# Transposed columns of the first image's lower half moved from the first stage into layer 0, and a step order of four for two images

## The chip, the cores and the metric

The kernel runs on one core of one Trainium2 chip. The metric is the device time of one execution in microseconds. Times "before" are of three runs; the profile is one more execution, taken by the hardware profiler.

## The reference, cut to what matters

The input x is 4 images of 16 channels, 256 x 256. Two layers, each a residual around a normalisation and a convolution:

```python
x = x + _L0_conv_ref(_gn(x), conv_w, conv_b)
x = x + _L1_conv_ref(_gn(x), base_w, spline_w, spline_scaler, bias)

def _L0_conv_ref(x, conv_w, conv_b):          # x is already normalised
    out = conv3x3(x, conv_w) + conv_b         # 16*25 output channels
    weights = softmax(out.reshape(N, C, 25, H, W), axis=2)
    return einsum('ncuij,ncuij->ncij', unfold5x5(x), weights)

def _gn(v, G=8, eps=1e-5):                    # over pairs of channels of an image
    g = v.reshape(B, G, C // G, H, W)
    return ((g - mean(g)) / sqrt(var(g) + eps)).reshape(v.shape)
```

Layer 1 is a 3 x 3 convolution of spline features and of silu of the normalised x. The change doesn't touch it.

## The kernel before, in words

**First stage (L404 to L589).** All 8 half images (4 images, 128 rows each) are loaded (`load_x`, L415; the two halves of image 0 stay in `held`, the others share three buffers). For each half DVE takes the statistics (L534, L536), ACT the squares (L543), PE sums them (L546), DVE takes the maximum (L549). After each image `group_stats` gives mean and deviation (with one power on POOL, L154). After the last image a flag is made (L580 to L589) which bounds the logits; every engine branches on it, and one of two equal arms runs (L1116).

Beside this the first image is normalised by the generator `normalize` (L264), two or three steps of which are taken after each piece of the statistics (L540, L541, L550). The order of instructions on each engine in this stage is chosen by a scheduler from what the program issues; it is not the order of the source.

**What `normalize` makes.** It works through four groups of four channels (q). `rows(q)` (L317) makes, for each half h, two forms of the normalised x on ACT: `hsp`, strips with a border of two columns (L327), stored in `hs` by `put_rows`, and `ht`, the same values reordered for the transposes (L340). `columns(q, n, h)` (L349) makes one tile of the transposed image: four PE transposes to PSUM (`tp`, L362), a copy `tt` (by DVE in the first stage, by ACT otherwise, L355), a copy `hi` rounded to float32r (ACT, L355), and the difference `lo` = `tp` - `hi` (DVE, L370). Each tile has 130 rows: a half with one row of the other half as border, for which 128x4 copies are made (L357, L359, and `border`, L311, for `lo`). There are 4 x 2 x 2 tiles for an image. `put_columns` (L294) stores `tt`, `hi`, `lo` of both halves in `hst` and `hsl`, six stores of 260 KB for each (q, n). Stores and loads are put in a list `moves` with the number of steps by which they are late. In this kernel a tile takes six steps: transposes, copies, difference, three empty ones.

Images 1, 2 and 3 are normalised in the same way during the layer 0 of the image ahead of them; there x comes into two tiles `xp` (`load`, L278), one for each half.

**Layer 0 (L620 to L883).** 64 strips (4 images, 2 halves, 8 strips of 32 columns), 8 steps of four columns each. In a step PE makes the logits (L833 from `am`, which is read from `hst`; L837 from `an`, which is read from `hsl`), ACT the exponentials `e` (L856), POOL the products with the neighbourhood `u`, read from `hs` (L861), DVE the sums of numerators and denominators (`nd`, L700), one step later. `e` has four buffers, `lg` three, `am`/`an` three; an `am` block serves two steps and is loaded two blocks ahead (L819). Once a strip DVE divides (L720 to L722), POOL subtracts (L728). After that comes one step of `normalize` (L870). Within layer 0 each engine's instructions run in the order of the source (`in_order`, L591). All these loads and stores are issued by SP on one queue.

**Layer 1 (L886 to L1110)** follows on all engines.

Of the kernel before, what the change touches and what calls it, by code (L numbers as in the profile page):

```python
# [3 lines left out]

# [7 lines left out]
F32 = mybir.dt.float32  # L12
F32R = mybir.dt.float32r
AF = mybir.ActivationFunctionType
# [20 lines left out]
def conv_preact_kernel(  # L35
# [12 lines left out]
    nc = tc.nc  # L48
    B, C, H, W = x.shape
    G = 8  # L50
    GC = C // G
    P = 128
    NH = H // P
# [3 lines left out]
    PAD = K // 2  # L57
# [3 lines left out]
    SW = 32  # L61
    NST = W // SW
    SP = SW + 2 * PAD
# [4 lines left out]
    RP = P + 2  # L68
    CT = (W + 2) * RP
    QC = 4  # L70
    QW = W // (P // QC)
    QG = 4
# [8 lines left out]
    const = ctx.enter_context(tc.tile_pool(name="const", bufs=1))  # L81
# [42 lines left out]
    for r in range(RT):  # L124
        p = P // 2 + SROWS.index(r + 1) * C
# [118 lines left out]
    zpad = const.tile([P, QC, PAD], F32, name="zpad")  # L244
    nc.vector.memset(zpad, 0.0)

    def zeros(b, queue):

        for e in (0, HP - PAD):
            for r in range(PAD):  # L250
                yield partial(
                    queue.dma_start,
                    hs[b][:, e + r].rearrange("s c w -> c s w"),
                    zero[0:C, 0 : NST * SP].rearrange("c (s w) -> c s w", s=NST),
                )
        for h in range(NH):
            for w in (0, (W + 1) * RP):
                yield partial(queue.dma_start, hst[b][h][:, w : w + RP], zero[0:C, 0:RP])
                yield partial(
                    queue.dma_start,  # L260
                    hsl[b][h][:, :, w : w + RP].rearrange("c t r -> (c t) r"), zero[:, 0:RP],
                )

    def normalize(b, ptr, tiles, held=None, copier=None):  # L264

        prep, xps, tts, his, los = tiles
        copier = copier or nc.scalar.copy

        moves = [(20 + 4 * i, f) for i, f in enumerate(zeros(b, nc.sync))] if held is None else []

        def move():
            for f in [f for i, f in moves if i <= 0]:
                f()
            moves[:] = [(i - 1, f) for i, f in moves if i > 0]

        def load(q, h):  # L278
            if held is None and q < C // QC:
                nc.sync.dma_start(  # L280
                    xps[h][:, :, PAD : PAD + W],
                    x[b, q * QC : (q + 1) * QC, h * P : (h + 1) * P, :].rearrange(
                        "c p w -> p c w"),
                )

        def put_rows(q, h, hsp):
            r0 = PAD + h * P
            nc.sync.dma_start(
                hs[b][:, r0 : r0 + P, q * QC : (q + 1) * QC, :].rearrange(
                    "s r c w -> r s (c w)"),  # L290
                hsp.rearrange("p s c w -> p s (c w)"),
            )

        def put_columns(q, n):  # L294
            g0 = n * QG
            for h in range(NH):
# [13 lines left out]

        def border(t):  # L311
            nc.scalar.copy(t[:, 1, :, 0:1], t[:, 0, :, P : P + 1])
            nc.scalar.copy(t[:, 0, :, RP - 1 :], t[:, 1, :, 1:2])

        hts = {}

        def rows(q):  # L317
            for h in range(NH):
                xp = xps[h] if held is None else held[h][:, q * QC : (q + 1) * QC]
                hsp = prep.tile([P, NST, QC, SP], F32, name=f"hsp{b}_{q}_{h}", tag="hsp")  # L320
                ht = prep.tile([P, QW, W // QW, QC], F32, name=f"ht{b}_{q}_{h}", tag=f"ht{h}")
                hts[q, h] = ht
                for k in range(QC // GC):
                    g = q * (QC // GC) + k
                    kc = slice(k * GC, (k + 1) * GC)
                    how = dict(scale=nrm[b][:, 0, g : g + 1], bias=nrm[b][:, 1, g : g + 1])
                    nc.scalar.activation(  # L327
                        hsp[:, :, kc, :].rearrange("p s c w -> p c s w"),
                        bass.AP(
                            tensor=xp.tensor, offset=xp.offset + k * GC * (W + 2 * PAD),  # L330
                            ap=[xp.ap[0], [W + 2 * PAD, GC], [SW, NST], [1, SP]],
                        ),
                        AF.Identity, **how,
                    )
                    if k == QC // GC - 1:
                        nc.scalar.copy(hsp[:, 0, :, 0:PAD], zpad)
                        nc.scalar.copy(hsp[:, NST - 1, :, PAD + SW :], zpad)
                        moves.append((4, partial(put_rows, q, h, hsp)))
                    yield
                    nc.scalar.activation(  # L340
                        ht[:, :, :, kc].rearrange("p g w c -> p c w g"),
                        xp[:, kc, PAD : PAD + W].rearrange("p c (w g) -> p c w g", g=QW),
                        AF.Identity, **how,
                    )
                    if k == QC // GC - 1:
                        moves.append((4, partial(load, q + 1, h)))
                    yield

        def columns(q, n, h):  # L349

            tp = ptr.tile([P, QG, P], F32, name=f"tp{b}_{q}_{n}_{h}", tag="tp")

            def copy(t, to):

                to(t[:, h, :, 1 : 1 + P], tp)  # L355
                if h == 0:
                    to(t[:, 1, :, 0:1], tp[:, :, P - 1 :])  # L357
                else:
                    to(t[:, 0, :, RP - 1 :], tp[:, :, 0:1])  # L359

            for k in range(QG):
                nc.tensor.transpose(  # L362
                    tp[:, k, :], hts[q, h][:, n * QG + k].rearrange("p w c -> p (w c)"), ident
                )
            yield
            copy(tts[n], copier)
            copy(his[n], nc.scalar.copy)
            yield

            nc.vector.tensor_sub(  # L370
                los[n][:, h, :, 1 : 1 + P], tp, his[n][:, h, :, 1 : 1 + P].bitcast(F32)
            )
            if h == NH - 1:
                moves.append((5, partial(border, los[n])))
                moves.append((9, partial(put_columns, q, n)))
            yield
            yield
            yield
            yield

        for h in range(NH):
            load(0, h)
        yield
        for _ in rows(0):
            move()
            yield
        for q in range(C // QC):
            ahead = rows(q + 1) if q + 1 < C // QC else iter(())
            for n in range(QW // QG):
                for h in range(NH):  # L390
                    for k, _ in enumerate(columns(q, n, h)):
                        if k % 3 == 2:
                            next(ahead, None)
                        move()
                        yield
            for _ in ahead:
                move()
                yield
        while moves:
            move()  # L400
            yield


    with tc.tile_pool(name="prep0", bufs=2) as prep, tc.tile_pool(  # L404
# [121 lines left out]
        for b in range(B):  # L526
# [44 lines left out]
            if b == 1:  # L571
                prepare1()
            if b == 0:
                ahead = normalize(0, ptr0, tiles, held, nc.vector.tensor_copy)
                next(ahead)
        for _ in ahead:
            pass
# [42 lines left out]
    def layer0(shift):  # L620
# [4 lines left out]
        with tc.tile_pool(name=f"prep{arm}", bufs=2) as prep, tc.tile_pool(  # L625
# [172 lines left out]
            for n, (b, hf, s) in enumerate(strips):  # L798
                if (hf, s) == (0, 0):
                    for _ in ahead:  # L800
                        pass
                    ahead = normalize(b + 1, ptr, tiles) if b + 1 < B else iter(())
                    if b == B - 1:
                        bank = ptr.tile([P, QG, P], F32, name=f"ps{arm}", tag="tp")
                        first_scales = [scales(k, partial(lambda k: bank[:, k], k)) for k in range(2)]
                last = (hf, s) == (NH - 1, NST - 1)
                if last:
                    for _ in ahead:
                        pass
                u = us.pop(0)  # L810
                if s * SW % CX == 0:
# [350 lines left out]
```

## Time and profile before

| | |
|---|---|
| median of three runs | 3069.55 us |
| lowest, highest | 3064.12, 3075.65 us |
| the profiled execution, own time | 3061.86 us |
| its span, first to last instruction | 3059.8 us |
| DVE busy in the span | 2959.0 us (97%) |
| PE busy in the span | 2802.6 us (92%) |
| ACT, POOL busy | 2236.6 us (73%), 1947.6 us (64%) |
| moved by DMA | 626.29 MB |

Times in the trace count from the span's start. A group of instructions is shown as line, engine, operation, output and inputs by the program's names, shapes and count, then the busy time in us and the mean of one in ns, then the idle time of the engine just before them and what ended it. `PEld` is PE's loading of weights. In a list of waits, the columns are who waited for whom, the sum in us, how often, and the longest. The share of DMA is the mean busy share of the core's 16 DMA engines, which can be a little over 1 by the packets' own records.

### The profile page before, as it was taken

The page shows a single profiled execution, that of the slowest core. Times are in us where ns is not written, and L with a number is a line of the kernel's source. Part 1 is how long each engine was busy: PE and PEld are TensorE (multiplying, and loading weights), DVE is VectorE, ACT ScalarE, POOL GpSimd, SP SyncE. Part 2 cuts the span into 40 slices and gives each one's busy share as a digit, 9 for nine tenths or more (in the row PEclk, how much of TensorE's full clock was granted, in tenths as well). Part 3 has the DMA queues.
Part 4 walks back from the last instruction along what each step waited for, and adds up shares of the span by engine and source line. Part 5 has one row for each costly group of instructions (what it writes and reads, how often), then busy time and mean ns, then how long its engine had stood idle before and what let it go on. Part 6 is the DMA issues. An engine that isn't in the chain of part 4 may idle for free.

```text
span 3059.8 us, 39743 instructions
## 1 busy us (share of the span) xinstructions
PE 2802.6 (92%) x14248; PEld 1448.2 (47%) x14248; DVE 2959.0 (97%) x1587; ACT 2236.6 (73%) x2587; POOL 1947.6 (64%) x744
## 2 busy tenths in 40 slices
PE   4499999999999999999999999958999999999998
PEld 3366656656656666666666566632222222222222
DVE  7599999999999999999999999998999999999997
ACT  6466765676766566766646546559999999999996
POOL 4199999999999999999999999980100100000000
PEclk7699999999999999999999999978999999999999
DMA  8988977879878778978767667659999999999994
GB/s 273 290 223 221 258 205 209 222 189 257 234 209 240 196 202 225 248 216 220 212 174 200 164 173 194 161 131 198 201 192 195 198 194 189 198 194 202 190 197 91
DMA packets 350929, 626.29 MB, mean 205 GB/s; under 512 B 41330, under 2 KB 216676, under 8 KB 334852
## 3 DMA queue, kind: packets, MB, share of 16 engines
q1 hardware_dynamic: 318020, 605.29, 81.0%
q10 hardware_dynamic: 30960, 15.73, 1.8%
q0 software_dynamic: 1744, 2.64, 0.3%
q8 instruction: 117, 1.92, 0.3%
q14 instruction: 88, 0.72, 0.1%
HBM read 513.95 MB, written 104.24 MB: 202 GB/s over the span
## 4 chain that ended last, share of the span: by engine, by line
DVE 69%; issue 11%; PE 8%; DMA 3%; ACT 3%; POOL 2%; SPq 1%; DVEq 0%; ACTq 0%; POOLq 0%
DVE nd L700 44%; PE lg L833 6%; DVE ta L168 4%; DVE ta L167 4%; DVE tb L168 4%; DVE tb L167 4%; DVE tb L158 2%; PE lg L837 1%; DVE yo L1020 1%; POOL e L861 1%; DVE r L721 1%; DVE nd L720 1%; DVE lo L370 1%; DMA am<-hst 1%; DVE nd L722 1%
## 5 line engine op out<-in xcount | busy, mean ns | idle before, releaser
L861 POOL TENSOR_TENSOR e<-e,u 128x1600 f32<-128x1600 f32 x512 | 1788.4, 3539 | 49.0 <-ACT e L856 30.9
L833 PE MATMUL lg<-wm,am 128*128 128x400 f32 x4096 | 1734.8, 505 | 83.8 <-ACT e L856 53.0
L700 DVE TENSOR_REDUCE nd<-e 128x128 f32<-128x3200 f32 x512 | 1748.0, 3478 | 29.0 <-POOL e L861 28.9
L837 PE MATMUL lg<-wn,an 97*128 97x400 f32 x2048 | 1344.9, 657 | 17.3 <-DMA an<-hsl 17.3
L856 ACT ACTIVATE e<-lg 128x800 f32<-128x800 f32 x1024 | 818.2, 837 | 708.9 <-DVE nd L700 460.5
L833 PEld LDWEIGHTS lg<-wm,am 128*128 128x128 f32 x4096 | 760.9, 192 | 403.3 <-ACT e L856 98.2
L1037 PE MATMUL yp<-ring,wt 128*32 128x512 f32 x6144 | 745.9, 598 | 87.6 <-DVE ring L169 63.7
L837 PEld LDWEIGHTS lg<-wn,an 97*128 97x128 f32 x2048 | 388.3, 190 | 334.5 <-issue 23.6
L1037 PEld LDWEIGHTS yp<-ring,wt 128*32 128x32 f32 x6144 | 203.7, 109 | 621.7 <-issue 427.7
L954 POOL MEMSET sl<- 16x256 f32 x6 | 1.8, 306 | 402.7 <-ACT ta L163 299.8
L169 DVE SCALAR_TENSOR_TENSOR ring<-ta,ta 128x2048 f32<-128x2048 f32 (+1 forms) x64 | 147.9, 2310 | 2.5
L168 DVE TENSOR_TENSOR ta<-ta,ta 128x2048 f32<-128x2048 f32 (+1 forms) x64 | 147.5, 2305 | 2.8 <-ACT ta L166 2.8
L169 DVE SCALAR_TENSOR_TENSOR ring<-tb,tb 128x2048 f32<-128x2048 f32 x64 | 145.6, 2275 | 2.5
L748 ACT ACTIVATE z<-xc,nrm 128x256 f32<-128x256 f32 x240 | 144.2, 601 | 5.3 <-POOL xc L728 1.2
L168 DVE TENSOR_TENSOR tb<-tb,tb 128x2048 f32<-128x2048 f32 x64 | 145.4, 2271 | 0.0
L1047 PE MATMUL yp<-sl,ws 64*32 64x512 f32 (+1 forms) x1032 | 131.3, 602 | 0.0
L954 POOL MEMSET slc<- 16x256 f32 x2 | 0.6, 307 | 203.1 <-ACT ta L163 203.0
L166 ACT ACTIVATE ta<-ta 128x2048 f32<-128x2048 f32 (+1 forms) x64 | 123.4, 1928 | 2.0
L193 POOL TENSOR_TENSOR d<-d,nrz 128x8 f32<-128x8 f32 x4 | 2.7, 669 | 191.8 <-DVE d L191 191.8
L166 ACT ACTIVATE tb<-tb 128x2048 f32<-128x2048 f32 x64 | 120.6, 1884 | 0.0
L973 ACT ACTIVATE sl<-sl,q 64x2048 f32<-64x2048 f32 x43 | 90.0, 2094 | 1.1
L728 POOL TENSOR_TENSOR xc<-xc,nd 128x512 f32<-128x512 f32 x64 | 82.5, 1289 | 8.2 <-DVE nd L722 8.2
(195 smaller groups left out, 2089.3 us busy)
## 6 DMA issues: line engine op xcount, KB each, us to landing
am<-hst SPq DMA_DIRECT2D x512, 194.6 KB
u<-hs SPq DMA_DIRECT2D x320, 288.0 KB
an<-hsl SPq DMA_DIRECT2D x512, 129.8 KB
xta<-x1s SPq DMA_DIRECT2D x40, 1024.0 KB
xtb<-x1s SPq DMA_DIRECT2D x40, 1024.0 KB
xtc<-x1s SPq DMA_DIRECT2D x40, 1024.0 KB
am<-hst SPq DMA_DIRECT2D x256, 129.8 KB
sl<-x1s SPq DMA_DIRECT2D x166, 128.0 KB
```

The lines of the kernel that those rows point to most:

```text
L166: nc.scalar.activation(s1, r1, AF.Square, scale=2.0)
L167: nc.vector.scalar_tensor_tensor(s2, t, 2.0, s2, ALU.subtract, ALU.mult)
L168: nc.vector.tensor_mul(s1, s1, r1)
L169: nc.vector.scalar_tensor_tensor(f, s2, 0.0, s1, ALU.min, ALU.subtract if given else ALU.add)
L700: nc.vector.tensor_reduce(nd[:, :, :, j : j + JG].rearrange("p t c j -> p t j c"), e.rearrange("p t j m c d -> p t j c m d"), AX.XY, ALU.add,)
L748: nc.scalar.activation(z, v, f, scale=nrm[b][:, 0, g : g + 1], bias=nrm[b][:, 1, g : g + 1], accum_out=st1[b][:, t, g, columns_of(n) : col ...
L833: nc.tensor.matmul(lg[:, i, :NL], lhsT=am[:, o : o + P], rhs=wm.rearrange("p m c d -> p (m c d)"), start=True, stop=False,)
L837: nc.tensor.matmul(lg[:, i, :NL], lhsT=an[:, o : o + P], rhs=wn.rearrange("p m c d -> p (m c d)"), start=False, stop=True,)
L856: nc.scalar.activation(ev, lg[:, :, :NL], AF.Exp)
L861: nc.gpsimd.tensor_tensor(e[:, 1].rearrange("p j m c d -> p j (m c) d"), e[:, 0].rearrange("p j m c d -> p j (m c) d"), uv, ALU.mult,)
L1037: nc.tensor.matmul(yp[t * M : (t + 1) * M], lhsT=wt[:, d, e].rearrange("p r o -> p (r o)"), rhs=ring[:, r0 + t * RT + d : r0 + t * RT + d ...
L1047: nc.tensor.matmul(yp[t * M : (t + 1) * M], lhsT=ws[v, e].rearrange("p r o -> p (r o)"), rhs=sl[n % 3][v, t : t + NT + 1 : NT, e : e + W], ...
```

## The change

`normalize` gets a `part`: None is the whole image, 0 and 1 are the two halves of image 0. In the first stage only part 0 runs: it makes rows and `ht` of both halves and transposes both, but of the lower half's tiles it takes only the border row; the upper half's border row, which the lower half will need, is kept in three small tiles (`kept`, for `tt`, `hi`, `lo`). Part 1 runs in layer 0 of image 0, ahead of image 1's normalisation: it loads the lower half of image 0 again, four channels at a time into the two `xp` tiles in turn and two groups ahead, makes `ht`, transposes, copies, takes the difference and stores three pieces for a tile. With `dense` (part 1, and image 1) transposes, copies and difference of a tile are issued in one step, followed by three empty ones, and a step of `rows` comes in every second step. Images 2 and 3 keep six steps. Stores of part 1 are issued four steps after the difference, not nine.

```diff
+    NQ = QW // QG
+    kept = [
+        const.tile([P, C // QC * NQ, QG, 1], d, name=f"kept{i}") for i, d in enumerate((F32, F32R, F32R))
+    ]
-    def normalize(b, ptr, tiles, held=None, copier=None):
+    def normalize(b, ptr, tiles, held=None, copier=None, part=None, dense=False):
-        moves = [(20 + 4 * i, f) for i, f in enumerate(zeros(b, nc.sync))] if held is None else []
+        moves = [(20 + 4 * i, f) for i, f in enumerate(zeros(b, nc.sync))]
+        moves = moves if held is None and part is None else []
+        parts = range(NH) if part is None else (part,)
+        read = range(NH) if part != 1 else (1,)
+        def place(q, h):
+            return xps[h if part is None else q % 2]
...
-                    xps[h][:, :, PAD : PAD + W],
+                    place(q, h)[:, :, PAD : PAD + W],
...
         def put_columns(q, n):
-            for h in range(NH):
+            for h in parts:
...
         def rows(q):
-            for h in range(NH):
-                xp = xps[h] if held is None else held[h][:, q * QC : (q + 1) * QC]
+            for h in read:
+                xp = place(q, h) if held is None else held[h][:, q * QC : (q + 1) * QC]
...
+                    if part != 1:
                         (hsp as before, with its yield)
...
-                        moves.append((4, partial(load, q + 1, h)))
+                        moves.append((4, partial(load, q + (1 if part is None else 2), h)))
...
-            def copy(t, to):
-                to(t[:, h, :, 1 : 1 + P], tp)
-                if h == 0:
-                    to(t[:, 1, :, 0:1], tp[:, :, P - 1 :])
+            def copy(t, to, keep):
+                if h in parts:
+                    to(t[:, h, :, 1 : 1 + P], tp)
+                if part == 1:
+                    to(t[:, 1, :, 0:1], keep[:, q * NQ + n])
+                elif h == 1:
+                    to(t[:, 0, :, RP - 1 :], tp[:, :, 0:1])
                 else:
-                    to(t[:, 0, :, RP - 1 :], tp[:, :, 0:1])
+                    to(t[:, 1, :, 0:1] if part is None else keep[:, q * NQ + n], tp[:, :, P - 1 :])
...
-            yield
-            copy(tts[n], copier)
-            copy(his[n], nc.scalar.copy)
-            yield
+            if not dense:
+                yield
+            copy(tts[n], copier, kept[0])
+            copy(his[n], nc.scalar.copy, kept[1])
+            if not dense:
+                yield
+            v = slice(1, 1 + P) if h in parts else slice(RP - 1, RP)
+            to = h if h in parts else 0
             nc.vector.tensor_sub(
-                los[n][:, h, :, 1 : 1 + P], tp, his[n][:, h, :, 1 : 1 + P].bitcast(F32)
+                los[n][:, to, :, v], tp[:, :, 0 : v.stop - v.start],
+                his[n][:, to, :, v].bitcast(F32),
             )
+            if part == 0 and h == 0:
+                moves.append((1, partial(
+                    nc.scalar.copy, kept[2][:, q * NQ + n], los[n][:, 0, :, P : P + 1]
+                )))
+            if part == 1:
+                nc.scalar.copy(los[n][:, 1, :, 0:1], kept[2][:, q * NQ + n])
             if h == NH - 1:
-                moves.append((5, partial(border, los[n])))
-                moves.append((9, partial(put_columns, q, n)))
+                if part is None:
+                    moves.append((5, partial(border, los[n])))
+                moves.append((9 if part is None else 4, partial(put_columns, q, n)))
...
-        for h in range(NH):
+        for h in read:
             load(0, h)
+            if part == 1:
+                load(1, h)
         yield
+        if part == 1:
+            yield
...
-                        if k % 3 == 2:
+                        if k in ((1, 3) if dense else (2, 5)):
                             next(ahead, None)
...
-                ahead = normalize(0, ptr0, tiles, held, nc.vector.tensor_copy)
+                ahead = normalize(0, ptr0, tiles, held, nc.vector.tensor_copy, 0)
...
-                    ahead = normalize(b + 1, ptr, tiles) if b + 1 < B else iter(())
+                    ahead = normalize(b + 1, ptr, tiles, dense=b == 0) if b + 1 < B else iter(())
+                    if b == 0:
+                        late = normalize(0, ptr, tiles, part=1, dense=True)
+                        ahead = chain(late, ahead)
...
+                if n == NST - 2:
+                    for _ in late:
+                        pass
```

Lines are those of the kernel before; in the changed kernel the same code stands up to 45 lines later.

More of the change, by code (lines that the diff above doesn't have):

```diff
@@ L2 @@
 from functools import partial
+from itertools import chain
 from itertools import chain
@@ L317, in rows @@
         def rows(q):
-            for h in range(NH):
-                xp = xps[h] if held is None else held[h][:, q * QC : (q + 1) * QC]
-                hsp = prep.tile([P, NST, QC, SP], F32, name=f"hsp{b}_{q}_{h}", tag="hsp")
+            for h in read:
+                xp = place(q, h) if held is None else held[h][:, q * QC : (q + 1) * QC]
+                if part != 1:
+                    hsp = prep.tile([P, NST, QC, SP], F32, name=f"hsp{b}_{q}_{h}", tag="hsp")
                 ht = prep.tile([P, QW, W // QW, QC], F32, name=f"ht{b}_{q}_{h}", tag=f"ht{h}")
@@ L326, in rows @@
                     how = dict(scale=nrm[b][:, 0, g : g + 1], bias=nrm[b][:, 1, g : g + 1])
[L327 to L338, printed above, removed]
-                    yield
+                    if part != 1:
+                        nc.scalar.activation(
+                            hsp[:, :, kc, :].rearrange("p s c w -> p c s w"),
+                            bass.AP(
+                                tensor=xp.tensor, offset=xp.offset + k * GC * (W + 2 * PAD),
+                                ap=[xp.ap[0], [W + 2 * PAD, GC], [SW, NST], [1, SP]],
+                            ),
+                            AF.Identity, **how,
+                        )
+                        if k == QC // GC - 1:
+                            nc.scalar.copy(hsp[:, 0, :, 0:PAD], zpad)
+                            nc.scalar.copy(hsp[:, NST - 1, :, PAD + SW :], zpad)
+                            moves.append((4, partial(put_rows, q, h, hsp)))
+                        yield
                     nc.scalar.activation(
@@ L364, in columns @@
                 )
-            yield
-            copy(tts[n], copier)
-            copy(his[n], nc.scalar.copy)
-            yield
+            if not dense:
[6 more added lines that the diff above has]
+            to = h if h in parts else 0
             nc.vector.tensor_sub(
-                los[n][:, h, :, 1 : 1 + P], tp, his[n][:, h, :, 1 : 1 + P].bitcast(F32)
-            )
+                los[n][:, to, :, v], tp[:, :, 0 : v.stop - v.start],
+                his[n][:, to, :, v].bitcast(F32),
+            )
+            if part == 0 and h == 0:
[4 more added lines that the diff above has]
+                nc.scalar.copy(los[n][:, 1, :, 0:1], kept[2][:, q * NQ + n])
             if h == NH - 1:
-                moves.append((5, partial(border, los[n])))
-                moves.append((9, partial(put_columns, q, n)))
+                if part is None:
+                    moves.append((5, partial(border, los[n])))
+                moves.append((9 if part is None else 4, partial(put_columns, q, n)))
             yield
@@ L379, in columns @@
             yield
-        for h in range(NH):
+        for h in read:
             load(0, h)
+            if part == 1:
+                load(1, h)
         yield
+        if part == 1:
+            yield
         for _ in rows(0):
@@ L389, in normalize @@
             for n in range(QW // QG):
-                for h in range(NH):
+                for h in read:
                     for k, _ in enumerate(columns(q, n, h)):
-                        if k % 3 == 2:
+                        if k in ((1, 3) if dense else (2, 5)):
                             next(ahead, None)
```

## The prediction

> **What bounds the kernel now.** I read the page's slices first, then the same by stretches of 50 us (columns: stretch, then busy us and count of PE, PEld, DVE, ACT, POOL, then granted clock, DMA share, GB/s).
>
> ```profile
> DMA  8988977879878778978767667659999999999994
> ```
> ```profile
> 50.00:100.00 50.00, 27.16 (x115) 22.57 (x115) 38.19 (x111) 43.79 (x63) 3.71 (x4) 0.60 0.90 293
> 100.00:150.00 50.00, 21.70 (x77) 14.15 (x76) 21.60 (x54) 13.32 (x30) 9.87 (x21) 0.67 1.02 284
> 200.00:250.00 50.00, 50.00 (x182) 33.11 (x181) 49.93 (x20) 33.83 (x54) 50.00 (x16) 1.00 0.91 245
> 1650.00:1700.00 50.00, 47.50 (x166) 30.55 (x165) 49.86 (x22) 23.83 (x34) 50.00 (x16) 1.00 0.64 160
> ```
> To 150 us (statistics and the first image's normalisation) the 16 DMA engines are full and no engine is; from 160 to 2040 us (layer 0) DVE has no gap, with POOL and PE close behind. The groups of DVE in one image's layer 0 (165 to 640 us) and all waits of layer 0 say the same: DVE never waits, and what others wait for is mostly DVE.
>
> ```profile
> L700 DVE TENSOR_REDUCE nd<-e 128x128 f32<-128x3200 f32 x128 | 437.2, 3478 | 0.1
> L370 DVE TENSOR_TENSOR lo<-tp,hi 128x512 fp32r<-128x512 f32 x16 | 10.9, 681 | 0.0
> ```
> ```profile
> ACT e L856 <- DVE nd L700: 460.5, 298, 4.5
> ...
> PE lg L833 <- DMA am<-hst: 14.3, 7, 5.2
> ```
> Then the timeline between the stages, by engine (start, length, what, idle before and its releaser).
>
> ```profile
> 120.44 1.87 SPq L648 DMA_DIRECT2D am<-hst  x3
> ...
> 129.75 5.59 SPq L648 DMA_DIRECT2D am<-hst  x1
> ```
> ```profile
> 135.04 0.84 ACT L856 ACTIVATE e<-lg 128x800 f32<-128x800 f32 x1 [0.87 <-PE lg L837]
> 147.17 0.87 ACT L327 ACTIVATE hsp<-xp,nrm 128x576 f32<-128x576 f32 x1 [11.30 <-DMA am<-hst]
> ```
> ```profile
> 136.91 6.97 DVE L700 TENSOR_REDUCE nd<-e 128x128 f32<-128x3200 f32 x2 [16.95 <-POOL e L861]
> 153.11 3.49 DVE L700 TENSOR_REDUCE nd<-e 128x128 f32<-128x3200 f32 x1 [9.23 <-POOL e L861]
> 157.03 3.49 DVE L700 TENSOR_REDUCE nd<-e 128x128 f32<-128x3200 f32 x1 [0.43 <-POOL e L861]
> 161.04 13.96 DVE L700 TENSOR_REDUCE nd<-e 128x128 f32<-128x3200 f32 x4 [0.53 <-POOL e L861]
> ```
> Layer 0's loads begin at 120.44. ACT stands 11.3 us after two steps of exponentials: its next instruction reads the x tiles of image 1 (named am in the wait, but the instruction reads xp), whose loads are behind 3 of am/an, one of u and 1 MB of xc. DVE runs without a break from 161.04 only.
>
> **What the Trainium skill says.** "Perfetto Trace Analysis", section Optimization Strategy: where the most contended engine changes over time, interleaving the regimes may help. The trace agrees on the regimes (DMA 1.02 before 150 us, DVE 49.9 of 50 after), not yet on the gain. The same page, Optimizing Scalar/DVE Operations: the profiled latency holds a half that overlaps the next instruction; here a difference shows 0.68 us, but the next starts 0.60 us after it (below), so I charge 0.60. "DMA: Bandwidth & Descriptors", Issuing engines are not separate DMA queues: all transfers share 16 engines and interleave, so moved stores meet the am loads; the loads already wait for PE or each other, and PE waits 14.3 us for am in 1,880.
>
> **The change, part by part.**
>
> *Taken from the first stage.* For the lower half's 8 tiles: 8 DVE copies and 8 differences, 8 ACT roundings, and 24 stores of 260 KB. The 32 transposes stay there, for the border column (128x4 copies of 0.06 us start to start). DVE: 8 x (0.60 + 0.60) = 9.6 us; ACT: 8 x 0.50 = 4.0 us; stores: 6.4 MB, at the 337 GB/s of 60 to 120 us, 19 us. No one of these is the gain: none is alone on the path. I follow the chain instead, with durations of before and the built order of the changed kernel:
> - SP stood from 45.4 to 59.2 for hsp with stores queued behind it; now the first group of stores is ahead of it. The load of the seventh x half goes out at about 61.5 instead of 64.9 and has fewer stores before it: landed at 72 instead of 75.9.
> - The last x half had 12 stores between it and that load; now 3, so it goes out at about 74 instead of 84.7 and lands at 84 instead of 95.
> - Arrival then no longer decides; ACT's row does: squares of the sixth, seventh and eighth half (3.5 us each) with 1.2 us `ht`, 0.8 us `hsp` and 0.5 us roundings end at about 75, 84 and 91 (before 79.6, 87.2, 99.1).
> - PE's sums of squares at half clock with two transposes between (5.4 us before), held about 3 us by differences that free PSUM: maximum at about 99.6 (before 102.9). From there to the flag 10.5 us in before, less a copy, a difference and a wait for a rounding, 2.8: 107.3 (before 113.4).
> - After the flag came one more tile and 6 stores, to 119.0; now the last stores are out before the flag. First load of layer 0 at about 108 instead of 120.4: 12.5 us. Bounds: 6 (the flag's gain alone) and 17 (stores' DMA time nearly in full).
>
> *The start of layer 0.* Loads keep their order, and image 0's lower x takes the place of image 1's. But in ACT's row no `hsp` comes, and the first `ht` stands after six exponentials, not two, and needs one x tile, not both. The tile lands 23.4 us after the first load (26.7 before, less 2.4 for the second and 0.9 of old stores). `ht` 1.1, two exponentials 1.6, POOL 3.5, the fourth sum 3.5: the fifth sum starts 33.7 us after the first load; before, 161.04 - 120.44 = 40.6. Gain 6.9 us; bounds 2 and 9.
>
> *Added in image 0's layer 0.* 8 differences on DVE, which has no gap: 8 x 0.60 = 4.8 us, all on the path. Copies and roundings go to ACT (8 x 1.3 us, and `ht` 8 x 1.1: 19 us in image 0, where ACT is busy 34 of 50 and otherwise waits for DVE). PE: 32 transposes, 8 x 0.44 = 3.5 us, under its 2 to 4 idle us in 50. SP: 24 stores and 4 loads of 512 KB, 28 x 0.6 = 17 us of issue, under its 548 us of waiting for PE's release of am. If these covers were gone they would cost up to 19, 3.5 and 17 us.
> DMA: 8.5 MB, 25 us at the same rate. Without normalisation the share in layer 0 is about 0.69 (four stretches from 1650: 0.60 to 0.74), in image 0 about 0.85; the difference over an image is some 67 us. Image 1's normalisation now fills about 80 steps of 3.75 us, not 105: 67/300 = 0.22 more, so 0.91. The windows show up to 1.0 without a gap on DVE: cost 0, bounds 0 and 8.
>
> *One step of four.* No instruction more for image 1. New waits: ACT's copies wait for transposes of the same step, DVE's difference for ACT's rounding of the same step. Behind the difference on DVE stands the next sum. The timeline has the distance (the same tile from the transposes to the difference):
>
> ```profile
> 301.42 0.60 PE L362 MATMUL tp<-ident,ht 128*128 128x128 f32 x4
> ...
> 309.28 0.59 ACT L355 CAST hi<-tp 128x512 fp32r<-128x512 f32 x1
> ...
> 321.43 0.68 DVE L370 TENSOR_TENSOR lo<-tp,hi 128x512 fp32r<-128x512 f32 x1
> 322.03 10.26 DVE L700 TENSOR_REDUCE nd<-e 128x128 f32<-128x3200 f32 x3
> ```
> The rounding is done 11.6 us ahead of the difference. One step (3.65) earlier for ACT, two for DVE leave 8 us: cost 0. Transposes reuse PSUM four steps after the difference, as now. On SP the lower half's stores come 4 steps after their difference; next am loads stand behind them, due two blocks (14.6 us) later: cost 0, bounds 0 and 4.
>
> **Sum.** -12.5 - 6.9 + 4.8 = -14.6 us. The profiled execution (span 3059.8, own time 3061.86) becomes 3047.3; the median of the runs, 3069.55, lies 7.7 above it, and becomes 3055. Own range -24 to -4: 3045 to 3065.
>
> **The rivals.** *The first stage doesn't end earlier:* x loads and statistics set it, stores were a shadow. For: SP's stalls are partly ACT's; against: full DMA and the tail after the flag. Only the start's 6.9 remains, less 4.8: 3067. *Crowded DMA:* at 0.91 the am loads come late in bursts; if a tenth of the 67 + 25 us shows on PE and gets through, 9, with the 8 of the bounds above: about -14.6 + 15, 3070. *Same-step waits (slower):* if ACT's lead is below zero at the differences, each of 24 tiles stops DVE for transposes 0.6, copies 1.2 and part of an exponential 0.7: 24 x 2.5 = 60 us, 3115. It decides only once 8 us of lead are lost, for example behind a late store that still reads `hi`.
>
> **How the numbers follow.** Forecast 0.76, no earlier end 0.08, crowded DMA 0.08, same-step waits 0.08. 0.5% is 15.3 us, about what a measurement of this kernel can tell from no change. The forecast's centre is 0.7 us inside that, and what I left at zero lies rather on the gain's side (am and u also land earlier without old stores ahead of them), so a little over half of its 0.76 goes beyond: faster 0.42. The rest, 0.34, and the next two cases, 0.16, make within 0.50; slower 0.08. Range: 3044 to 3070, the last case left out.
>
> **What would show it.** Right: the first am load near 108 us, ACT's first `ht` after six exponentials, DVE gapless from about 142, the same spacing to 2040, an am wait no larger. Wrong: a difference that waits for ACT, PE waiting for am above 15 us, a first load after 115.

## The result, and the profile after

| | before | changed | ratio, 95% interval |
|---|---|---|---|
| median of the runs, us | 3066.84 (3061.70 to 3075.65, 4 runs) | 3047.90 (3045.66 to 3052.85, 4 runs) | 0.9945 [0.9923, 0.9967] |
| the profiled execution: own time / span, us | 3061.86 / 3059.8 | 3052.85 / 3050.8 | one execution each: -9.0 |

The kernel is faster by 19 us in these runs, and by 9 us in the two profiled executions. That is one finding, not two: in these runs the executions of before lie up to 14 us apart, those of the changed kernel 7 us. So the changed kernel was run twice more without an edit, on two different chips, each time beside the kernel before:

| | changed | before | ratio, 95% interval |
|---|---|---|---|
| first repeat | 3049.14 (6 runs) | 3062.06 (43 runs) | 0.9953 [0.9937, 0.9968] |
| second repeat | 3051.24 (12 runs) | 3061.45 (49 runs) | 0.9972 [0.9960, 0.9985] |

The gain is 10 to 19 us by chip (13 and 10 in the repeats), 0.3 to 0.55%. The forecast was 14.6.

Now the views that answer to those of before. First the page's slices (busy share of the DMA engines in 40 slices) and two stretches (stretch, busy us and count of PE, PEld, DVE, ACT, POOL, granted clock, DMA share, GB/s), changed kernel:

```profile
DMA  8988988878978778878857667659999999999993
```
```profile
100.00:150.00 50.00, 33.19 (x100) 20.18 (x100) 25.47 (x40) 18.33 (x27) 23.69 (x25) 0.80 0.88 230
200.00:250.00 50.00, 50.00 (x185) 33.17 (x183) 49.86 (x23) 30.39 (x50) 50.00 (x16) 1.00 0.88 253
```

The regimes are what they were: DVE fills layer 0 (49.9 of 50). What differs is the stretch from 100 to 150 us, in which PE works 33.2 us instead of 21.7 and POOL 23.7 instead of 9.9: layer 0 begins earlier in it. Then SP's queue, ACT and DVE between the stages, changed kernel (start, length, what, idle before and its releaser):

```profile
108.56 1.88 SPq L686 DMA_DIRECT2D am<-hst  x3
...
117.71 0.41 SPq L716 DMA_DIRECT2D xc<-in_x_dram  x1
119.11 5.78 SPq L686 DMA_DIRECT2D am<-hst  x3
```
```profile
134.99 1.27 ACT L359 ACTIVATE ht<-xp,nrm 128x512 f32<-128x512 f32 x1 [6.36 <-DMA am<-hst]
```
```profile
107.31 0.14 DVE L627 CAST flag<-bd 1x1 int32<-1x1 f32 x1
...
124.16 6.97 DVE L738 TENSOR_REDUCE nd<-e 128x128 f32<-128x3200 f32 x2 [12.44 <-POOL e L906]
132.27 3.49 DVE L738 TENSOR_REDUCE nd<-e 128x128 f32<-128x3200 f32 x1 [1.14 <-POOL e L906]
141.27 3.49 DVE L738 TENSOR_REDUCE nd<-e 128x128 f32<-128x3200 f32 x1 [5.51 <-POOL e L906]
144.68 0.68 DVE L396 TENSOR_TENSOR lo<-tp,hi 128x512 fp32r<-128x512 f32 x1
145.28 3.48 DVE L738 TENSOR_REDUCE nd<-e 128x128 f32<-128x3200 f32 x1
149.86 10.48 DVE L738 TENSOR_REDUCE nd<-e 128x128 f32<-128x3200 f32 x3 [1.11 <-POOL e L906]
```

The first load of layer 0 goes out at 108.56 instead of 120.44. ACT's first `ht` stands after six exponentials, as built, and still waits 6.4 us for its x (the wait is named `am`, but the instruction reads `xp`; 11.3 before). DVE's longest break after its first sums is 5.5 us, ahead of the fourth sum; before it was 9.2, ahead of the third. The fifth sum starts at 145.28 instead of 161.04. Last the groups of DVE in image 0 (150 to 625 us) and the waits of all of layer 0 (total us, times, longest), changed kernel:

```profile
L738 DVE TENSOR_REDUCE nd<-e 128x128 f32<-128x3200 f32 x127 | 434.8, 3478 | 2.5 <-POOL e L906 2.5
L396 DVE TENSOR_TENSOR lo<-tp,hi 128x512 fp32r<-128x512 f32 x23 | 15.7, 681 | 0.0
```
```profile
ACT e L901 <- DVE nd L738: 440.7, 290, 4.5
...
PE lg L878 <- DMA am<-hst: 16.0, 8, 5.0
...
ACT hsp L346 <- DMA xp<-in_x_dram: 9.5, 3, 4.2
...
DVE nd L738 <- POOL e L906: 5.2, 6, 1.2
```

The differences have become 23 in this window (the 24th is the one at 144.68), with no idle time ahead of any: none waits for ACT. A line that before did not have is `hsp` waiting for `xp`: where image 1's normalisation begins in the middle of image 0, ACT stands for x.

**Where the time came from.** Shifts of three executions of the changed kernel against the profiled one of before, in us, taken from the starts on SP and DVE:

| | first load | fifth sum | image 1's first sum | last sum of layer 0 | end |
|---|---|---|---|---|---|
| changed | -11.9 | -15.8 | -9.1 | -8.0 | -9.1 |
| first repeat | -12.1 | -17.9 | -13.1 | -13.8 | -15.6 |
| second repeat | -12.5 | -20.4 | -12.5 | -10.8 | -11.0 |
| denser steps alone (an experiment below) | -1.1 | -4.3 | -4.6 | -4.5 | -4.0 |

Against this one execution, all three win 12 us in the first stage and 4 to 8 more by the fifth sum, and give 5 to 8 back in image 0. After image 0 they move by 2.4 us at most.

The last row shows how far one execution of before can be trusted as the zero. Up to the fifth sum the rows of all engines in that kernel's trace are those of before, instruction by instruction, and yet:

```profile
119.35 1.87 SPq L686 DMA_DIRECT2D am<-hst  x3
```
```profile
149.36 3.49 DVE L738 TENSOR_REDUCE nd<-e 128x128 f32<-128x3200 f32 x1 [7.29 <-POOL e L905]
153.28 20.91 DVE L738 TENSOR_REDUCE nd<-e 128x128 f32<-128x3200 f32 x6 [0.43 <-POOL e L905]
```

Its fifth sum (the second of the last row; it starts at 156.76) is 4.3 us earlier than in before, with nothing done for it. Counted from this execution the changed kernel wins 10.8 to 11.4 us in the first stage, but only 0.7 to 4.8 more by the fifth sum. The first stage stands firm: in four executions with the old first stage (two of them from the experiments on the kernel before) the first load goes out at 119.0 to 120.4, in eight with the new one, experiments included, at 108.0 to 109.4, which is 11.1 us apart on average.

### The profile page after: what moved, and what is told of

Read it like the earlier page. It is cut to its first block, busy times and chain, and to the rows that moved or that the text cites. A ratio compares the mean times of both kernels' runs of the same rounds, so it can differ in the third digit from the quotient of the medians.

```text
span 3050.8 us, 39867 instructions
## 1 busy us (share of the span) xinstructions
PE 2804.2 (92%) x14280; PEld 1447.6 (47%) x14280; DVE 2954.8 (97%) x1587; ACT 2252.1 (74%) x2619; POOL 1948.5 (64%) x744
## 4 chain that ended last, share of the span: by engine, by line
DVE 68%; issue 12%; PE 9%; DMA 5%; ACT 3%; POOL 2%; SPq 1%; DVEq 0%; POOLq 0%; ACTq 0%
DVE nd L738 43%; PE lg L878 6%; DVE ta L169 4%; DVE ta L168 4%; DVE tb L169 4%; DVE tb L168 4%; DVE tb L159 2%; PE lg L882 2%; DVE yo L1065 1%; POOL e L906 1%; DVE r L759 1%; DMA an<-hsl 1%; DVE nd L758 1%; DVE nd L760 1%; DVE lo L396 1%
## 5 line engine op out<-in xcount | busy, mean ns | idle before, releaser
L882 PE MATMUL lg<-wn,an 97*128 97x400 f32 x2048 | 1344.3, 656 | 12.8 <-DMA an<-hsl 12.7
L882 PEld LDWEIGHTS lg<-wn,an 97*128 97x128 f32 x2048 | 388.1, 190 | 330.7 <-issue 21.7
```

The costliest lines, as they stand in the source:

```text
L882: nc.tensor.matmul(lg[:, i, :NL], lhsT=an[:, o : o + P], rhs=wn.rearrange("p m c d -> p (m c d)"), start=False, stop=True,)
```

## The experiments

Theory: three terms, as predicted: an earlier end of the first stage, an earlier unbroken row on DVE because ACT asks later for x, less eight differences on DVE. Rivals: the whole gain is the place of ACT's wait, and the first stage a side matter; the denser steps cost or win something by themselves; the stores alone, or the engines' work alone, set the end of the first stage. Each kernel was run in five rounds beside the kernel before.

**The changed kernel again** (first repeat, in the tables above).

> The changed kernel once more, against the kernel before in five rounds, since two profiled executions gave -9 us and the medians of four runs -19. Sum of the forecast's terms as measured in the first trace (first load of layer 0 11.9 us earlier, start of layer 0 2.8 better, 8 differences 4.8, gaps of DVE 1.4): ratio 0.997. If the medians are right: 0.994.

Measured 0.9953 [0.9937, 0.9968]. What follows: differences of a few us between the times of single executions mean nothing. The readings below are mostly of starts on SP and DVE early in the trace, and even these carry the spread shown above.

**Denser steps for image 1 alone**, first stage and image 0 as before:

```diff
-                ahead = normalize(0, ptr0, tiles, held, nc.vector.tensor_copy, 0)
+                ahead = normalize(0, ptr0, tiles, held, nc.vector.tensor_copy)
...
-                        late = normalize(0, ptr, tiles, part=1, dense=True)
-                        ahead = chain(late, ahead)
+                        late = iter(())
```

> Only the step order of four for image 1, nothing moved out of the first stage. If a same-step wait cost 2.5 us a tile, 16 tiles make +40 us (ratio 1.013). My theory: no difference on DVE waits for ACT, ratio 1.000 within 0.002, and the sums of image 0 keep the spacing of the kernel before to within 1 us.

Measured 0.9992 [0.9981, 1.0002] (3059.75 against 3062.06). From the sixth sum to image 1's first, image 0 takes 457.9 us, before 458.2. One step of four by itself costs nothing that these runs can tell, and no difference waits for ACT.

**The lower half's work back in the first stage, without its stores** (eight DVE copies, eight roundings, eight differences, made and not used):

```diff
-                if h in parts:
+                if h in parts or part == 0:
                     to(t[:, h, :, 1 : 1 + P], tp)
...
+            if part == 0 and h == 1:
+                nc.vector.tensor_sub(
+                    los[n][:, 1, :, 1 : 1 + P], tp, his[n][:, 1, :, 1 : 1 + P].bitcast(F32),
+                )
```

> The changed kernel, with the lower half's 8 copies, 8 roundings and 8 differences made in the first stage as well (their result is not used), but not its 24 stores. If the engines' work set the end of the first stage, the first load of layer 0 goes back from 108.6 us to about 116 to 120. If the stores did, it stays within 2 us of 108.6. I expect something between, nearer to the work: 114, 5 us above the changed kernel.

Measured 0.9972 [0.9962, 0.9982], 3053.56, 4.4 above the changed kernel on the same chip (the two intervals overlap a little). The flag and the first load, this kernel:

```profile
112.23 0.14 DVE L631 CAST flag<-bd 1x1 int32<-1x1 f32 x1
```
```profile
113.49 1.87 SPq L690 DMA_DIRECT2D am<-hst  x3
```

The first load is 4.9 to 5.5 us later than in the three executions of the change alone, and so is the flag: it comes 4.9 us later than in the first of them.

**The stores back, without the work** (24 stores of the upper tiles a second time, into spare memory):

```diff
+    spare = dram.tile([C, CT], F32, name="spare"), dram.tile([C, 2, CT], F32, name="sparel")
...
-            for h in parts:
+            for h in range(NH) if part == 0 else parts:
...
-                    d = to[b][h]
+                    d = to[b][h] if h in parts else spare[int(to is hsl)]
```

> The changed kernel, with 24 stores of 260 KB more in the first stage, where the lower half's stood, into spare memory (the upper half's tiles a second time), but without the work of the engines for them. If the stores set the end of the first stage: the first load of layer 0 goes back to 117 to 120 and lands later still, 12 us or more above the changed kernel. If the work did: first load within 3 us of 108.6, and at most 3 us more by old stores ahead of the loads. I expect 114 and 7 us.

Measured 0.9997 [0.9985, 1.0009]: the gain is gone. The flag and SP's queue of this kernel at the end of the first stage:

```profile
108.64 0.14 DVE L628 CAST flag<-bd 1x1 int32<-1x1 f32 x1
```
```profile
109.58 0.52 SPq L320 DMA_DIRECT2D hst<-tt  x1
...
114.73 0.60 SPq L320 DMA_DIRECT2D sparel<-lo  x1
116.93 1.88 SPq L687 DMA_DIRECT2D am<-hst  x3
```

The flag is ready at 108.64, only 1.3 us later than with the change, but the last six stores still go out after it, and layer 0's loads stand behind them on SP: 116.93, later by 8.4. So the stores act as a tail after the flag, the work acts through the flag. 4.9 + 8.4 = 13.3 against the 11.9 of the change: both are needed for it, and the stores weigh more. The runs as a whole lost more (12 us) than the first stage explains: the trace also has short breaks on DVE in layer 1, between 2135 and 2375 us, some 8 us, with at most 1.5 there in any other trace. There ACT waits eight times, 7.8 us in all, for `sl` to be loaded from `x1s`; in that stretch of the first repeat it does not. Why these loads are late isn't known; the spare tensors move other tensors in memory, and that was not tried separately. The 8.4 us are read from the trace, not from the ratio.

**Part 1's rows three steps later**, so that ACT asks still later for x:

```diff
         if part == 1:
-            yield
+            for _ in range(4):
+                yield
```

> The changed kernel, with the lower half's rows three steps later (its loads of x stay where they are), so that ACT's first reordering of x stands after twelve exponentials, not six. My theory: DVE's gap before the fourth sum (5.5 and 4.1 us in the two traces of the changed kernel) is ACT standing for x; it goes, and the time falls by 4 us, to a ratio of 0.994 to the kernel before. Rival: the am blocks arrive too late anyway, and the gap only moves to the next sums: no gain.

Measured 0.9958 [0.9945, 0.9971] (3051.11, 5 runs). DVE at the start of layer 0, this kernel:

```profile
124.81 20.89 DVE L739 TENSOR_REDUCE nd<-e 128x128 f32<-128x3200 f32 x6 [12.99 <-POOL e L907]
```

Six sums stand back to back; the break ahead of the fourth has gone. The sixth sum is 22.3 us earlier than in before, in the three executions without the edit 14.7, 17.7 and 20.5; the last sum of layer 0 is 17.1 earlier, without the edit 8.0, 13.8 and 10.8. The break went, as the theory says. A gain in time is not shown: the runs don't resolve it, and the profiled execution (3043.28 us) is the fastest of the five.

**The same in the kernel before**: image 1's rows four steps later, nothing else.

```diff
         yield
+        if b == 1:
+            for _ in range(4):
+                yield
         for _ in rows(0):
```

> The kernel before, with the normalisation of image 1 four steps later, its loads of x where they were. This is the second term of the forecast alone: ACT's 11.3 us of waiting for x leave the way of the exponentials. My theory: the 9.2 us gap of DVE before the third sum shrinks to below 2, the first load of layer 0 stays at 120.4, and the time falls by 7 to 8 us (ratio 0.9975). Rival: the am blocks set the gap: no change.

Measured 0.9970 [0.9960, 0.9980] (3054.30 against 3064.27). DVE of this kernel:

```profile
135.74 13.93 DVE L703 TENSOR_REDUCE nd<-e 128x128 f32<-128x3200 f32 x4 [15.99 <-POOL e L864]
150.27 6.97 DVE L703 TENSOR_REDUCE nd<-e 128x128 f32<-128x3200 f32 x2 [0.60 <-POOL e L864]
```

The first load stands at 120.35, as in before (120.44), and the 9.2 us break is gone; the sixth sum is earlier by 10.8, the last one by 9.8. Three lines that move no work win 10 us in these runs. So the rival that ACT's place in the row is a large part of the gain holds, as a share: it can be had without the change. How large is less sure: up to 4.3 of the 10.8 us can be the slow start of the one execution of before, and a later kernel with these three lines (the later xc in the kernel before) gained less. Whether the change wins beside it, two pairs say, given with that kernel.

**The changed kernel with part 1's rows three steps later, and the first 1 MB of xc loaded later** (that load stands ahead of the x loads on SP; it now goes out in the first strip):

```diff
-            nxc, xc = load_xc(0), None
+            nxc = xc = None
...
+                    if (n, j) == (0, CI):
+                        xc = load_xc(0)
                     if j == SW // 2:
```

> The kernel with the lower half's rows three steps later, and the first 1 MB load of xc, which nobody reads in the first strip, put behind the first four am blocks. If what is left at the start of layer 0 are am blocks behind xc, 2 to 3 us less than without (ratio 0.993 to the kernel before); if DVE has no gap left there, nothing more.

Measured 0.9947 [0.9933, 0.9962] (3044.78). It was run again, beside the changed kernel on one chip:

> The kernel with the lower half's rows three steps later and xc's first load behind the am blocks, beside the changed kernel on one chip. By the traces (the last sum of layer 0 at 2026.3 against 2030.2 and 2035.9) it is 4 to 9 us faster than the changed kernel; if the runs show less than 2, the start of layer 0 is not worth what its gap says.

Measured 0.9945 [0.9933, 0.9957] (3046.14), the changed kernel 0.9972 [0.9960, 0.9985] (3051.24). What was expected of that second repeat:

> The changed kernel beside the others of this call on one chip. Ratio to the kernel before 0.9953 as measured last; the spread of its start (DVE's gap before the fourth sum 4 or 5.5 us) stays.

This is the best version that keeps every term: 5 us below the changed kernel on the same chip, the intervals side by side without overlap. How much of this is the later rows and how much the later xc is not shown; beside the kernel with the later rows alone (0.9958) the intervals overlap. Its sixth sum is earlier than in before by 20.9 and 22.3 us in two executions, its last sum of layer 0 by 17.7 and 14.0.

**Before with later rows and the later xc**, to see whether xc wins anything alone:

> The kernel before with nothing moved out of the first stage: only the normalisation of image 1 four steps later, and xc's first load behind the am blocks. The wait alone gave 9.8 us in the trace and a ratio of 0.997. With xc later DVE should have no gap of over 1 us after its second sum: 1 to 3 us more, ratio 0.9965.

Measured 0.9988 [0.9979, 0.9998], where the later rows alone had given 0.9970 on another chip. Its trace has the sixth sum earlier by 11.1, the last one by 7.2. So no gain from xc is shown here, and rather a loss; the two were not run on one chip, and this stays open.

This kernel and the one before it differ by the change alone; in both, ACT passes twelve exponentials ahead of its first read of x. On one chip they took 3058.82 and 3046.14 us, and their intervals are far apart: 12.7 us for the change without its second term. In their traces the first load is 10.2 us earlier, the last sum of layer 0 6.8, the end 9.9. The other such pair, the two kernels with later rows and the old place of xc, has the first load 11.7 earlier and the last sum 7.3, but the medians are only 3.2 us apart (3054.30 and 3051.11) and the intervals overlap. In both pairs the last sum is 7 us earlier, about what the first stage leaves when the differences are paid (10.2 and 11.7 us less 4.8). So the first pair refutes the rival that ACT's place in the row is the whole gain.

**Part 1 without the difference** (ACT writes the transposes to `lo` in its place, so `lo` is not the rounding's rest and the logits lack their correction in the lower half of image 0):

> The changed kernel with the lower half's 8 differences left out: in their place ACT copies the transposed tile, so the low part of the lower half of image 0 is not what it should be. Price of the differences on DVE: 8 x 0.60 = 4.8 us, ratio 0.9937 to the kernel before if the changed one is 0.9953. If DVE had slack there, nothing.

Measured 0.9944 [0.9931, 0.9957] (3047.75, 5 runs). The differences in image 0 are down from 13.7 to 9.6 us, but image 0 takes 462.6 us from the sixth sum on, 463.8 with them.

DVE's breaks from the sixth sum on are 4.7 us here, and 2.4, 1.5 and 4.8 in the three executions with the differences, which take 463.8, 462.7 and 466.2 us. Those differ among themselves by as much as the 4.1 us saved, and the changed kernel itself did not run on this chip, so this experiment does not show what the differences cost. It also gives ACT eight copies more, and ACT waits 9.1 us for image 1's x just ahead of these breaks. The price is read better from the traces without their breaks: from the sixth sum to image 1's first, DVE then takes 461.2 to 461.4 us in the three executions of the changed kernel, 457.1 in before and 456.9 with the denser steps alone. That is 4.1 to 4.5 us for the seven differences that lie there, and 7 x 0.60 is 4.2.

**Part 1 dense, image 1 in the old six steps:**

```diff
-                    ahead = normalize(b + 1, ptr, tiles, dense=b == 0) if b + 1 < B else iter(())
+                    ahead = normalize(b + 1, ptr, tiles) if b + 1 < B else iter(())
```

> The changed kernel with six steps a tile for image 1, so that only the moved half is dense. Moved half and image 1 then need about 145 steps, of which 120 are there; what is left, some four tiles, is issued at once ahead of the last strip of image 0. Each of those tiles is then a chain of transposes, copies and difference with no sums between: I expect DVE gaps of 5 to 10 us near 575 us and a time 5 to 10 us above the changed kernel. If the engines run far enough ahead to hide it, no gap.

Measured 1.0020 [1.0010, 1.0029] (3068.74, 17.5 above the changed kernel on the same chip): more than expected. Image 1's last tiles no longer fit into image 0's steps; they are run out in one go (L850) ahead of image 0's last strip. DVE there, this kernel:

```profile
578.00 0.68 DVE L396 TENSOR_TENSOR lo<-tp,hi 128x512 fp32r<-128x512 f32 x1
581.13 0.69 DVE L396 TENSOR_TENSOR lo<-tp,hi 128x512 fp32r<-128x512 f32 x1 [2.45 <-ACT hi L379]
...
587.42 0.69 DVE L396 TENSOR_TENSOR lo<-tp,hi 128x512 fp32r<-128x512 f32 x1 [2.45 <-ACT hi L379]
588.02 3.48 DVE L738 TENSOR_REDUCE nd<-e 128x128 f32<-128x3200 f32 x1
595.42 10.46 DVE L738 TENSOR_REDUCE nd<-e 128x128 f32<-128x3200 f32 x3 [3.92 <-POOL e L906]
```

The one chain PE, ACT, DVE, PE with nothing beside it: 2.45 us of waiting for each of three tiles, and then 3.9 us until exponentials and products have caught up. DVE's breaks in image 0 make 16.9 us, with 1.5 to 4.8 in three executions of the changed kernel; these four waits hold 11.3 of them, the rest are short breaks at 319 to 323, 437 to 446 and 607 us. The 2.45 us are what the slower rival described (2.5 us a tile), at the one place where ACT has no lead. It also says what the denser steps are for: they make room, and part 1 costs more than it wins without them.

## Why the prediction was right

**The first stage: 12.5 us predicted; 11.9, 12.1 and 12.5 measured against one execution of before, 11.1 between the averages of all traces.** The first load was put at 108 and stands at 108.56; the flag was put at 107.3 and stands at 107.31. Two links on the way were off and cancelled, which is luck: the last x half went out at 77.2 rather than 74 and the squares ended at 94.3 rather than 91 (before 99.1). Yet the maximum came at 99.2, predicted 99.6, so PE's part after the squares took 4.9 us, not the 8.6 that the forecast gave it. What the prediction left open, how much of this is stores and how much work, the two halves show: 8.4 and 4.9 us, and the tail after the flag, which I named, is the larger.

**The start of layer 0: 6.9 us predicted.** The terms listed for it add up to 33.1 us, not 33.7, so they forecast 7.5. The fifth sum's shift, less the first load's, with the one difference that now lies ahead of that sum (0.6 us) put back, is 4.5, 6.4 and 8.6 us in three executions, inside the bounds of 2 and 9. Against the other execution of the old order it is 1.3, 3.2 and 5.4. So the sign is shown and the size is not, and that 6.9 comes near the first three is partly luck. (ACT's first read of x stood after four exponentials before, two steps of two, not after two; the change lets one step more pass.) The mechanism is the one named: ACT read x 26.4, 24.5 and 22.3 us after the first load (23.4 forecast), and still stood 6.4, 4.9 and 3.5 us for it. The edits that make ACT ask later, in both kernels, take the long break away. DVE's unbroken row begins at 149.9, 146.9 and 140.6 us, with 142 forecast.

**The differences: 4.8 us predicted.** 24 take 14.4 us in the kernel that holds all of them in the stretch counted, 16 take 9.6 in before: 0.60 each, as charged. "Perfetto Trace Analysis", section Optimizing Scalar/DVE Operations in the Trainium skill, says of the fixed data-access overhead of an instruction, for DVE about 60 ns on SBUF and 125 ns on PSUM, that the profiled latency holds about twice as much, and that the half for the write acknowledgement overlaps the next instruction. The trace agrees that such a part is there and that it is small: 0.08 us of the 0.68 shown. The measured spacing was the right price.

**What was put at nothing.** The rest, from the fifth sum to image 1's first, is 2.5, 0.6 and 3.7 us over those 4.8. It goes with breaks on DVE: 1.1 us ahead of the sixth sum in the first execution, and in image 0 mainly at 317 to 326 and at 557 to 565 us. The former follow ACT's wait of about 4 us for image 1's x near 300 us; the latter, about as long, follow waits of PE for `am` (1.9 and 4.6 us, near 548) and of POOL for its loads. I had 0, with bounds 0 and 8, and thought of `am` late for PE. That is there, and beside it x late for ACT, the same thing as at the start, one normalisation further on. Which wait ends in which break is read from their order in time and was not tried alone. PE's wait for `am` is 16.0 us (14.3 before): past the 15 that I had named as a sign against the forecast, without much harm, since DVE waits only 4.1 us from 160 us on (2.7 before), and all waits of PE and its loading for `am` and `an` fell from 46.3 to 40.6. The DMA share in image 0 is 0.87 on average over ten stretches of 50 us, with 0.91 predicted (the four stretches without normalisation average 0.67, not 0.69).

**The sum.** -12.2 for the first stage, -6.5 for the start, +4.8 for the differences and +2.3 for the breaks, the measured ones each a mean of three executions, make -11.6; the executions have -9.1, -13.1 and -12.5 at image 1's first sum, and the medians of the runs -19, -13 and -10. The -14.6 lies among the medians; it is 3 us too good against these traces, and 7 to 8 against the other execution of the old order, where the mean at image 1's first sum is -7.0. So the terms are shown, the sum only to several us.

**The rivals.** That the first stage doesn't end earlier is refuted by the first load. Crowded DMA happened in its small form, 1 to 4 us and not 15 (the 9 and 8 that its case adds up are 17). The same-step waits did not happen (no difference waits in the changed kernel; the denser steps alone take no time), and their price was right where they were forced.

## What to carry to other kernels

Where a stage ends with stores on the queue that the next stage's loads use, look at both what sets the flag and what is still queued after it; each half put back alone brought the next stage's first load 4.9 and 8.4 us back, and their sum is about the 11 to 12 us of both. Where an engine takes its instructions in order, look at the first instruction that reads a late load and count what useful work stands behind it: three lines that let ACT pass eight more exponentials first won 10 us of 3064 without moving any work, on one chip; with another edit beside them, on another chip, 3 us. Work moved to an engine without a gap is paid at its start-to-start spacing, and room must be made in its new place, or it is run out in one go.

## What the runs showed of the hardware

Not expected: executions of one file on one chip spread over 6 to 21 us of 3050, so a gain of 5 us was settled only by a pair on one chip.

Three loads of `am` took SP 5.8 us to issue (`119.11 5.78` above), three others 1.9 us. Full DMA engines alone are not the difference: the loads at 113.93 took 2.0 us at a share of about 1.0 too. Of the 5.8 us, 4.5 are the first load alone, and it stands directly behind the 1 MB load of xc. That is so in all of layer 0: in the profiled execution of the changed kernel the 11 loads of `am` issued directly behind one of xc took 3.0 to 4.7 us each, the other 757 had a median of 0.59 and none took over 1.8. Where xc was loaded later, the long issue moved with it:

```profile
128.91 0.39 SPq L717 DMA_DIRECT2D xc<-in_x_dram  x1
131.92 5.16 SPq L687 DMA_DIRECT2D am<-hst  x3
```

In the last row the first of the three takes 3.9 us; the three at 118.44, where the long issue was before, take 0.55 each. So a long issue on SP's row here is no sign of a long load: look at the one ahead of it, which shows 0.4 us for its 1 MB. Why it is so, no run shows.

And adding 24 stores to the first stage brought breaks of DVE 2,000 us later, in layer 1, with late loads of `sl` ahead of them; no experiment here explains those.
